# Group statistics by channel tiles on two engines, zeroing moved ahead, and a bias product moved behind the first products

## The chip, the cores and the metric

The kernel runs on one core of a Trainium2 chip. The time is the device time of one execution in microseconds. Engines are named as in the profile: PE (TensorE), DVE (VectorE), ACT (ScalarE), POOL (GpSimd) and SP, whose queue issues most of the DMAs.

## What is computed

Two layers on x of 384 channels by 192 by 192 pixels, in float32. Only the first half of the first layer bears on this change:

```python
def _gn(v, G=32, eps=1e-5):
    g = v.reshape(B_, G, C_ // G, H_, W_)
    m = jnp.mean(g, axis=(2, 3, 4), keepdims=True)
    s = jnp.var(g, axis=(2, 3, 4), keepdims=True)
    return ((g - m) / jnp.sqrt(s + eps)).reshape(v.shape)

x = x + L0(_gn(x))      # layer 0
x = x + L1(_gn(x))      # layer 1

# in L0, on h = _gn(x):
qkv = einsum('bchw,oc->bohw', h, w_qkv) + b_qkv      # 3*384 outputs
qkv = 2x2 max pool(qkv)                              # 96 x 96
qkv = depthwise 3x3 conv(qkv, w_dw) + b_dw
q, k, v = split(qkv)
attn = normalised q @ normalised k, over channels of a head
out = sum of four top-k softmaxes of attn @ v, gelu, repeat 2x2, projection
```

Layer 1 takes the sign of the normalised x, shifts channels by up to three columns and multiplies by the sign of a weight.

## The kernel before, in words

x is cut into 24 units of 8 image rows; a unit is 128 partitions by 3 channel tiles by 1536 pixels, 2304 KB. Units live in the pool "big" of eight slots (line 156), and `unit(u)` (lines 177 to 182) loads one by a DMA on SP's queue, or by three, one for each channel tile, with `parts=CT`.

Phase 1 (lines 219 to 294) streams all units, from 23 down to 0, and takes the statistics of the group norm. Every third unit goes to ACT whole: for each of its three channel tiles one pass that sums and one that sums the squares (line 239), into `acc`. The other units go to DVE whole: nine `bn_stats` of 512 pixels (line 248), and after every fourth such unit a `bn_aggr` for each tile (line 250). The last two units, 1 and 0, are both DVE's. Units 5 to 0 stay in their slots (`KEEP`). In between, nine matmuls of the group indicator with the weights (line 256) give `wg`, which ACT copies out (line 259). At the end DVE joins both kinds of partial sums (lines 263 to 269), PE adds them up by group (`group_sums`, line 198), a string of one-column steps makes mean and reciprocal deviation (lines 274 to 280), and `spread` (line 203) brings them back to channels. Then DVE scales the weights `wq` by the reciprocal deviation (line 287), nine matmuls of one column make the shift that the mean brings to the bias (line 293, "bqps"), and DVE adds it to `bq` (line 294). The normalised x is never written: the products take x itself, with the scaled weights.

Phase 2 (lines 353 to 436) makes q and k, unit by unit from 0 up. `qkv_unit` (lines 313 to 346) does one block of 128 output channels: three groups of three matmuls into a PSUM bank each (line 321, "qkv"; the pool has three banks), each group reduced by DVE's max pool (line 328) into a zero-bordered tile "pooled"; then ACT adds the bias `bq` (line 335) and begins the depthwise sum (line 342), and DVE adds eight more terms (line 344). DVE transposes the result in 32 by 32 blocks into "blocks" (line 383), DMAs on SP's queue move these into "room" (lines 396 and 401), a tile in one of the eight slots, and PE adds the products of q and k over pixels (line 412, "gram"), one unit behind. POOL zeroes "blocks" (line 361) and the borders of the six pooled tiles (lines 302 to 305) at the start of this phase.

Later phases make v, the softmaxes and the attention (lines 571 to 660), and the projection, layer 1 and the stores (from line 665); the change does not touch their code. One small step of theirs, a group sum of the projection's bias (lines 630 and 631, "bg"), depends on nothing but a constant.

The order within an engine's queue is set by a scheduler that works from the program's dependencies, outside the blocks marked `manual_schedule`; the engines then run their queues in order. Pools give out memory; a tile waits until what lay there before has been read.

Of the kernel before, what the change touches and what calls it, by code (L numbers as in the profile page):

```python
# [10 lines left out]
F32 = mybir.dt.float32  # L11
# [3 lines left out]
BF16 = mybir.dt.bfloat16  # L15
# [5 lines left out]
P = 128  # L21
# [126 lines left out]
def conv_preact_kernel(ctx: ExitStack, tc: tile.TileContext, a: dict, out: bass.AP):  # L148
# [58 lines left out]
    def right(name, bufs=1, stack=att):  # L207
        return stack.enter_context(tc.tile_pool(name=name, bufs=bufs, side="right"))
# [4 lines left out]
    gsb = ap.tile([P, CT, max(DN)], F32, name="gsb")  # L213
    osum = ap.tile([P, CT, NAB], F32, name="osum")
    aT = right("aT").tile([P, CT, C], F32, name="aT")
    wq = right("wq").tile([P, CT, 3 * C], F32, name="wq")


    kept = {}
    with tc.tile_pool(name="p1", bufs=1, side="right") as p1, tc.tile_pool(name="p1ps", bufs=2, space=PSUM) as psp:  # L220
        stats = [p1.tile([P, CT, BATCH * (UPX // 512) * 6], F32, name=f"stats{i}") for i in range(NB)]
        mv = p1.tile([P, CT, NB, 2], F32, name="mv")
        acc = p1.tile([P, CT, 2, NU // SHARE], F32, name="acc")
        wg = p1.tile([NG, 3 * C], F32, name="wg")
        seen = 0
        for i in range(NU):
            u = NU - 1 - i
            xt = unit(u, parts=CT if u in (0, NU - 1) else 1)
            if u < KEEP:
                kept[u] = xt  # L230
            if i == 0:
                nc.scalar.dma_start(small, a["small"])
                nc.scalar.dma_start(indT, a["indT"])
                nc.scalar.dma_start(wq, a["w_qkvT"].rearrange("(t p) o -> p t o", p=P))
            if i % SHARE == 0:
                for t in range(CT):
                    for k, f in enumerate((AF.Identity, AF.Square)):
                        junk = p1.tile([P, UPX], BF16, name="junk")
                        nc.scalar.activation(  # L239
                            junk, xt[:, t], f, accum_out=acc[:, t, k, i // SHARE : i // SHARE + 1]  # L240
                        )
            else:
                b, k = divmod(seen, BATCH)
                seen += 1
                for t in range(CT):
                    for j in range(UPX // 512):
                        at = (k * (UPX // 512) + j) * 6
                        nc.vector.bn_stats(stats[b][:, t, at : at + 6], xt[:, t, j * 512 : (j + 1) * 512])  # L248
                    if k == BATCH - 1:
                        nc.vector.bn_aggr(mv[:, t, b, :], stats[b][:, t, :])  # L250
            if u == NU // 2:

                for m in range(3):
                    ps = psp.tile([NG, C], F32, name="wgps")
                    for t in range(CT):
                        nc.tensor.matmul(
                            ps, ind[:, t, :], wq[:, t, m * C : (m + 1) * C], start=(t == 0), stop=(t == CT - 1)
                        )
                    nc.scalar.copy(wg[:, m * C : (m + 1) * C], ps)

        sums = p1.tile([P, CT, 2], F32, name="sums")
        more = p1.tile([P, CT, 2], F32, name="more")
        nc.vector.tensor_reduce(more, acc, AX.X, ALU.add)
        sq = p1.tile([P, CT, NB], F32, name="sq0")
        nc.vector.tensor_mul(sq, mv[:, :, :, 0], mv[:, :, :, 0])
        nc.vector.tensor_add(sq, sq, mv[:, :, :, 1])
        nc.vector.tensor_reduce(sums[:, :, 0], mv[:, :, :, 0], AX.X, ALU.add)
        nc.vector.tensor_reduce(sums[:, :, 1], sq, AX.X, ALU.add)
        nc.vector.scalar_tensor_tensor(sums, more, 1.0 / (BATCH * UPX), sums, ALU.mult, ALU.add)  # L269
        ps = psp.tile([NG, 2], F32, name="gsps")  # L270
        group_sums(ps, sums)

        gs = p1.tile([NG, 2], F32, name="gs")
        nc.vector.tensor_scalar_mul(gs, ps, BATCH / (NU * GRP))
        gv = p1.tile([NG, 2], F32, name="gv")
        nc.vector.tensor_scalar_mul(gv[:, 0:1], gs[:, 0:1], -1.0)
        var = p1.tile([NG, 1], F32, name="var")
        nc.vector.scalar_tensor_tensor(var, gs[:, 0:1], gv[:, 0:1], gs[:, 1:2], ALU.mult, ALU.add)
        nc.vector.tensor_scalar_add(var, var, 1e-5)
        inv_sqrt(p1, gv[:, 1:2], var, 1, "s0", NG)  # L280
        ps = psp.tile([P, CT, 2], F32, name="spread")
        spread(ps, gv)
        nc.vector.tensor_copy(rstd0, ps[:, :, 1])

        for c0, c1 in ((0, P), (P, 2 * C), (2 * C, 3 * C)):
            for t in range(CT):
                nc.vector.tensor_scalar_mul(wq[:, t, c0:c1], wq[:, t, c0:c1], rstd0[:, t : t + 1])
        nc.vector.tensor_copy(nmean0, ps[:, :, 0])
        shift = p1.tile([NG, 1], F32, name="shift")
        nc.vector.tensor_mul(shift, gv[:, 0:1], gv[:, 1:2])  # L290
        ps = psp.tile([P, NM], F32, name="bqps")
        for m in range(NM):
            nc.tensor.matmul(ps[:, m : m + 1], wg[:, m * P : (m + 1) * P], shift, start=True, stop=True)
        nc.vector.tensor_add(bq, bq, ps)  # L294

    def padded(pool, n):

# [8 lines left out]
            ts.append(t)  # L306
        return ts

    def rows(u):

        return (1 if u else 2), (PR if u < NU - 1 else PR + 1)

    def qkv_unit(pqkv, xt, u, m, pl, parts):


        x4 = xt.rearrange("p t (r w) -> p t r w", w=W)
        lo, hi = rows(u)
        for r0, nr, c0, ncol in BLOCKS:
            ps = pqkv.tile([P, 512], F32, name="qkv")
            for t in range(CT):  # L320
                nc.tensor.matmul(  # L321
                    ps,
                    wq[:, t, m * P : (m + 1) * P],
                    x4[:, t, r0 : r0 + nr, c0 : c0 + ncol],
                    start=(t == 0),
                    stop=(t == CT - 1),
                )
            nc.vector.tensor_reduce(  # L328
                pl[:, 2 + r0 // 2 : 2 + (r0 + nr) // 2, 1 + c0 // 2 : 1 + (c0 + ncol) // 2],
                ps.rearrange("p (i a j b) -> p i j a b", a=2, b=2, j=ncol // 2),  # L330
                AX.XY,
                ALU.max,
            )
        new = pl[:, 2 : 2 + PR, 1 : 1 + WP]
        nc.scalar.activation(new, new, AF.Identity, bias=bq[:, m : m + 1])  # L335
        for acc, r0, n in parts:
            acc2 = acc.rearrange("p (r w) -> p r w", w=WP)
            for k in range(9):
                r = lo - 1 + r0 + k // 3
                src = pl[:, r : r + n, k % 3 : k % 3 + WP]  # L340
                if k == 0:
                    nc.scalar.activation(acc2, src, AF.Identity, bias=bdw[:, m : m + 1], scale=wdw[:, m, 0:1])  # L342
                else:
                    nc.vector.scalar_tensor_tensor(acc2, src, wdw[:, m, k : k + 1], acc2, ALU.mult, ALU.add)  # L344
        if u < NU - 1:
            nc.scalar.copy(pl[:, 0:2, :], pl[:, PR : PR + 2, :])  # L346
# [3 lines left out]
    pqkv = products_of_x.enter_context(tc.tile_pool(name="qkv", bufs=3, space=PSUM))  # L350
    last_products = products_of_x.enter_context(ExitStack())
    pg = last_products.enter_context(tc.tile_pool(name="p2g", bufs=1, space=PSUM))
    with tc.tile_pool(name="p2w", bufs=1, side="right") as wp, tc.tile_pool(
        name="p2t", bufs=2, side="right"
    ) as tp:
        gram = [pg.tile([P, 512], F32, name=f"gram{t}") for t in range(CT)]


        size = -(-(PR + 1) * WP // P) * C
        blocks = wp.tile([P, 2, size], F32, name="blocks")  # L360
        nc.gpsimd.memset(blocks, 0.0)
        pool = padded(wp, 2 * CT)
        room = big.tile([P, CT, UPX], F32, name="room", tag="big").rearrange("p t n -> p (t n)")
        qkT = room[:, : 2 * size].rearrange("p (s n) -> p s n", s=2)

        def of_unit(u):
# [53 lines left out]
        for u in range(NU):  # L420
# [6 lines left out]
            n = hi - lo + 1  # L427
            for m in range(2 * CT):
                acc = tp.tile([P, (PR + 1) * WP], F32, name="dw")[:, : n * WP]
                qkv_unit(pqkv, xt, u, m, pool[m], [(acc, 0, n)])  # L430
                transposed(u, *divmod(m, CT), acc)
                sq = tp.tile([P, (PR + 1) * WP], BF16, name="sq", bufs=1)
                nc.scalar.activation(sq[:, : n * WP], acc, AF.Square, accum_out=ssq[:, m, u : u + 1])  # L433
                if u and m == CT - 1:
                    products(u - 1)
                if m % CT == CT - 1:
                    moved(u, m // CT)
# [420 lines left out]
```

## Time and profile before

| | |
|---|---|
| median of 4 runs | 2287.62 us (2287.54 to 2289.3) |
| the profiled execution | 2287.57 us, span 2285.8 us |
| mean granted clock of PE | 0.965 |
| x loads of the first stage | 25 units' worth, 58.98 MB, on SP's queue until 165 us; the DMA engines move 410 to 425 GB/s without a gap until 150 us |
| first product (L321) | 160.86 us |
| bn_stats (L248) | 144, 676 ns each by their records |
| ACT's passes (L239) | 48, 1482 ns each, and a read of the sum after each |
| bqps (L293) | 18 records, from 156.63 on, 3.97 us |
| POOL's zeroing of "blocks" (L361) | 2.66 us, from 160.72 on |

A float32 matmul stands in the trace as two records, so nine matmuls are 18. In the profile "L321 qkv<-xt,wq" means: line 321 writes qkv from xt and wq. In the slices each digit is a fortieth of the span (57 us), in tenths busy; PEclk is the clock that was granted to PE, in tenths of full speed. In the timeline the bracket behind a row gives how long the engine had been idle before it and what ended that. In the windows the columns after the length are the busy times of PE, PE's weight loads, DVE, ACT and POOL with their counts, then the granted clock, the DMA share and GB/s.

### The profile page before, as it was taken

The page shows a single profiled execution, that of the slowest core. Times are in us where ns is not written, and L with a number is a line of the kernel's source. Part 1 is how long each engine was busy: PE and PEld are TensorE (multiplying, and loading weights), DVE is VectorE, ACT ScalarE, POOL GpSimd, SP SyncE. Part 2 cuts the span into 40 slices and gives each one's busy share as a digit, 9 for nine tenths or more (in the row PEclk, how much of TensorE's full clock was granted, in tenths as well). Part 3 has the DMA queues.
Part 4 walks back from the last instruction along what each step waited for, and adds up shares of the span by engine and source line. Part 5 has one row for each costly group of instructions (what it writes and reads, how often), then busy time and mean ns, then how long its engine had stood idle before and what let it go on. Part 6 is the DMA issues. An engine that isn't in the chain of part 4 may idle for free.

```text
span 2285.8 us, 19474 instructions
## 1 busy us (share of the span) xinstructions
PE 2101.0 (92%) x6135; PEld 993.5 (43%) x6135; DVE 1903.1 (83%) x3269; ACT 819.4 (36%) x1418; POOL 211.9 (9%) x338
## 2 busy tenths in 40 slices
PE   1029999999999999999999979999999999989998
PEld 0014444444444444444444434444444444445554
DVE  4667888888888888888888878986787887889998
ACT  5532222222222222222222212225323233487775
POOL 0000000000000000000000000000000000276674
PEclk7559999999999999999999989999999999999999
DMA  9962222232222232222232222104222212289996
GB/s 398 418 261 61 65 64 70 69 98 70 66 64 71 69 98 70 65 64 70 70 96 71 65 48 84 41 24 183 83 83 73 93 42 83 83 334 404 421 413 249
DMA packets 208727, 300.30 MB, mean 131 GB/s; under 512 B 162000, under 2 KB 164848, under 8 KB 208624
## 3 DMA queue, kind: packets, MB, share of 16 engines
q1 hardware_dynamic: 197936, 243.46, 30.7%
q10 hardware_dynamic: 10688, 55.61, 6.0%
q8 instruction: 48, 0.79, 0.1%
q14 instruction: 55, 0.45, 0.1%
HBM read 213.68 MB, written 56.62 MB: 118 GB/s over the span
## 4 chain that ended last, share of the span: by engine, by line
PE 75%; DVE 12%; DMA 8%; ACT 2%; issue 1%; SPq 1%; ACTq 0%; POOLq 0%; POOL 0%; DVEq 0%
PE qkv L321 63%; DMA xt<-in_x_dram 7%; DVE chunk L344 5%; PE l1ps L743 4%; PE yps L559 3%; PE gram L412 3%; DVE pooled L328 2%; PE ops L594 2%; DVE xt L568 2%; DVE dw L344 1%; ACT signs L723 1%; DVE stats L248 1%; DMA out_dram<-xt 1%; ACT chunk L342 0%; ACT pooled L335 0%
## 5 line engine op out<-in xcount | busy, mean ns | idle before, releaser
L321 PE MATMUL qkv<-xt,wq 128*128 128x512 f32 x3888 | 1682.5, 594 | 0.3 <-DVE small L294 0.3
L321 PEld LDWEIGHTS qkv<-xt,wq 128*128 128x128 f32 x3888 | 736.7, 190 | 920.5 <-issue 824.6
L344 DVE SCALAR_TENSOR_TENSOR dw<-pooled,small,dw 128x384 f32<-128x384 f32 (+2 forms) x1152 | 708.9, 615 | 118.8 <-ACT dw L342 93.7
L328 DVE TENSOR_REDUCE pooled<-qkv 128x128 f32<-128x512 f32 x648 | 442.5, 684 | 72.3 <-PE qkv L321 71.8
L344 DVE SCALAR_TENSOR_TENSOR chunk<-pooled,small,chunk 128x384 f32<-128x384 f32 (+3 forms) x696 | 370.1, 545 | 74.7 <-ACT chunk L342 57.3
L346 ACT COPY pooled<-pooled 128x196 f32<-128x196 f32 x207 | 73.7, 356 | 764.4 <-DVE dw L344 543.0
L335 ACT ACTIVATE pooled<-pooled,small 128x384 f32<-128x384 f32 x216 | 133.0, 616 | 408.1 <-DVE pooled L328 400.6
L723 ACT ACTIVATE signs<-xt,nmean 64x1536 fp8e4<-64x1536 f32 x144 | 226.5, 1573 | 62.0 <-PE yps L559 50.7
L743 PE MATMUL l1ps<-signs,wb 128*128 128x384 fp8e4 x864 | 150.6, 329 | 5.7 <-POOL signs L715 4.5
L568 DVE SCALAR_TENSOR_TENSOR xt<-yps,small,xt 128x768 f32<-128x768 f32 x132 | 127.8, 1012 | 24.3 <-PE yps L559 19.7
L559 PE MATMUL yps<-chunk,wpr 128*128 128x384 f32 x396 | 136.5, 490 | 6.6 <-DVE xt L568 6.6
L751 DVE SCALAR_TENSOR_TENSOR xt<-l1ps,small,xt 128x768 f32<-128x768 f32 x144 | 135.6, 1008 | 6.3 <-ACT signs L723 4.0
L248 DVE BATCH_NORM_STATS2 stats<-xt 128x6 f32<-128x512 f32 x144 | 87.2, 676 | 60.4 <-DMA xt<-in_x_dram 60.4
L198 PE MATMUL gsps<-sums,small 128*32 128x2 f32 x6 | 0.5, 196 | 127.9 <-DVE sums L269 127.9
L433 ACT ACTIVATE sq<-dw 128x384 bf16<-128x384 f32 (+2 forms) x144 | 75.3, 523 | 117.0 <-DVE dw L344 117.0
L743 PEld LDWEIGHTS <-wb 128*128 128x128 fp8e4 x864 | 84.1, 97 | 73.4 <-issue 15.5
L302 POOL MEMSET pooled<- 128x196 f32 x9 | 2.4, 269 | 1172.2 <-DVE dw L344 1154.8
L342 ACT ACTIVATE dw<-pooled,small 128x384 f32<-128x384 f32 (+2 forms) x144 | 100.5, 698 | 2.3
L559 PEld LDWEIGHTS yps<-chunk,wpr 128*128 128x128 f32 x396 | 72.7, 190 | 62.0 <-PE yps L559 15.6
L239 ACT ACTIVATE junk<-xt 128x1536 bf16<-128x1536 f32 x48 | 71.1, 1482 | 51.4 <-DMA xt<-in_x_dram 50.3
L383 DVE STREAM_TRANSPOSE blocks<-dw 128x384 f32<-128x384 f32 (+1 forms) x144 | 82.0, 569 | 3.4
L412 PE MATMUL gram<-room 128*128 128x160 f32 (+3 forms) x438 | 68.1, 309 | 15.3 <-DMA room<-blocks 15.3
(117 smaller groups left out, 641.3 us busy)
## 6 DMA issues: line engine op xcount, KB each, us to landing
xt<-in_x_dram SPq DMA_DIRECT2D x83, 2304.0 KB, 12.6
out_dram<-xt ACTq DMA_DIRECT2D x19, 2304.0 KB, 14.5
room<-blocks SPq DMA_DIRECT2D x736, 36.0 KB, 2.0
xt<-in_x_dram SPq DMA_DIRECT2D x18, 768.0 KB, 8.6
out_dram<-xt ACTq DMA_DIRECT2D x9, 768.0 KB, 8.3
out_dram<-xt SPq DMA_DIRECT2D x6, 768.0 KB, 6.6
wq<-in_w_qkvT_dram ACTq DMA_DIRECT2D x1, 1728.0 KB, 14.9
room<-blocks SPq DMA_DIRECT2D x32, 48.0 KB, 2.1
```

The lines of the kernel that those rows point to most:

```text
L248: nc.vector.bn_stats(stats[b][:, t, at : at + 6], xt[:, t, j * 512 : (j + 1) * 512])
L321: nc.tensor.matmul(ps, wq[:, t, m * P : (m + 1) * P], x4[:, t, r0 : r0 + nr, c0 : c0 + ncol], start=(t == 0), stop=(t == CT - 1),)
L328: nc.vector.tensor_reduce(pl[:, 2 + r0 // 2 : 2 + (r0 + nr) // 2, 1 + c0 // 2 : 1 + (c0 + ncol) // 2], ps.rearrange("p (i a j b) -> p i j ...
L335: nc.scalar.activation(new, new, AF.Identity, bias=bq[:, m : m + 1])
L342: nc.scalar.activation(acc2, src, AF.Identity, bias=bdw[:, m : m + 1], scale=wdw[:, m, 0:1])
L344: nc.vector.scalar_tensor_tensor(acc2, src, wdw[:, m, k : k + 1], acc2, ALU.mult, ALU.add)
L412: nc.tensor.matmul(gram[t][:, : BN[t] * B], q[:L, t, i], k[:L, B0[t] : B0[t] + BN[t], i], start=u == 0 and i == 0, stop=u == NU - 1 and i ...
L559: nc.tensor.matmul(ps, wpr[:, t, m * P : (m + 1) * P], o[:, t, :], start=(t == 0), stop=(t == CT - 1),)
L568: nc.vector.scalar_tensor_tensor(x5[:, m, r], yb, bpr[:, m : m + 1], x5[:, m, r], ALU.add, ALU.add)
L723: nc.scalar.activation(rows_of(sg, p, SAT[t] - HSHIFT[t][h]), xt[p, t, :].rearrange("p (r w) -> p r w", w=W), AF.Sign, bias=nmean1[p, t : ...
L743: nc.tensor.matmul(ps[:, j, : 2 * W], wb[:, t, m * P : (m + 1) * P], rows_of(sg, slice(0, P), SAT[t])[:, r0 + 2 * j : r0 + 2 * j + 2], sta ...
L751: nc.vector.scalar_tensor_tensor(blk, ps[:, :, : 2 * W], bl1[:, m : m + 1], blk, ALU.add, ALU.add)
```

## The change

- Statistics: of every unit one channel tile (number u modulo 3) goes to ACT and two go to DVE; both write into one tile `part`, ACT with its scale folded in, and one column of `part` carries the epsilon. The joining becomes a square, an add and one reduction; one scaling reads the sums from PSUM directly, and the step that added epsilon is gone. Unit 1 is loaded in three DMAs as well.
- Memory: the partial statistics and ACT's throwaway output lie in "room", which is now taken from the eight slots ahead of the stream; `wg` lies in `aT`, a tile of a later phase, and `shift` in a pool of its own.
- Zeroing: "blocks" and the six pooled tiles are allocated and zeroed ahead of the statistics.
- Bias: the nine matmuls and the add are a function that `qkv_unit` calls once, for unit 0 and block 0, behind the nine products and their three reductions, into a fourth tile of the product pool.
- The scheduler also moves "bg": its three matmuls and its DVE step now stand at the front of their queues. Otherwise the queues keep their order from the first products on.

```diff
+    wg = aT.rearrange("p t c -> p (t c)")[:NG]
+    shift = ap.tile([NG, 1], F32, name="shift")
...
-        stats = [p1.tile([P, CT, BATCH * (UPX // 512) * 6], F32, name=f"stats{i}") for i in range(NB)]
-        mv = p1.tile([P, CT, NB, 2], F32, name="mv")
-        acc = p1.tile([P, CT, 2, NU // SHARE], F32, name="acc")
-        wg = p1.tile([NG, 3 * C], F32, name="wg")
...
+    blocks = wp.tile([P, 2, size], F32, name="blocks")
+    nc.gpsimd.memset(blocks, 0.0)
+    padded_qk = padded(wp, 2 * CT)
+    room = big.tile([P, CT, UPX], F32, name="room", tag="big").rearrange("p t n -> p (t n)")
...
+        stats = [room[:, i * size1 : (i + 1) * size1].rearrange("p (t n) -> p t n", t=CT) for i in range(NB)]
+        junk = room[:, NB * size1 : NB * size1 + UPX // 2].bitcast(BF16)
+
+        part = p1.tile([P, CT, 2, NB + NU // SHARE + 1], F32, name="part")
+        measure = 1.0 / (BATCH * UPX)
+        nc.vector.memset(part[:, :, 0, NB + NU // SHARE :], 0.0)
+        nc.vector.memset(part[:, :, 1, NB + NU // SHARE :], 1e-5 * NU / BATCH)
...
-            xt = unit(u, parts=CT if u in (0, NU - 1) else 1)
+            xt = unit(u, parts=CT if u in (0, 1, NU - 1) else 1)
...
-            if i % SHARE == 0:
-                for t in range(CT):
-                    for k, f in enumerate((AF.Identity, AF.Square)):
-                        junk = p1.tile([P, UPX], BF16, name="junk")
-                        nc.scalar.activation(
-                            junk, xt[:, t], f, accum_out=acc[:, t, k, i // SHARE : i // SHARE + 1]
-                        )
-            else:
...
+            for t in range(CT):
+                if t == u % SHARE:
+                    at = NB + i // SHARE
+                    for k, f, scale in ((0, AF.Identity, measure), (1, AF.Square, measure**0.5)):
+                        nc.scalar.activation(junk, xt[:, t], f, scale=scale, accum_out=part[:, t, k, at : at + 1])
+                    continue
+                b, k = divmod(seen[t], BATCH)
+                seen[t] += 1
+                for j in range(UPX // 512):
+                    at = (k * (UPX // 512) + j) * 6
+                    nc.vector.bn_stats(stats[b][:, t, at : at + 6], xt[:, t, j * 512 : (j + 1) * 512])
+                if k == BATCH - 1:
+                    nc.vector.bn_aggr(part[:, t, :, b], stats[b][:, t, :])
...
-        nc.vector.tensor_reduce(more, acc, AX.X, ALU.add)
...
-        nc.vector.tensor_reduce(sums[:, :, 0], mv[:, :, :, 0], AX.X, ALU.add)
-        nc.vector.tensor_reduce(sums[:, :, 1], sq, AX.X, ALU.add)
-        nc.vector.scalar_tensor_tensor(sums, more, 1.0 / (BATCH * UPX), sums, ALU.mult, ALU.add)
...
+        nc.vector.tensor_mul(sq, part[:, :, 0, :NB], part[:, :, 0, :NB])
+        nc.vector.tensor_add(part[:, :, 1, :NB], part[:, :, 1, :NB], sq)
+        nc.vector.tensor_reduce(sums, part, AX.X, ALU.add)
...
-        nc.vector.tensor_scalar_mul(gv[:, 0:1], gs[:, 0:1], -1.0)
+        nc.vector.tensor_scalar_mul(gv[:, 0:1], ps[:, 0:1], -BATCH / (NU * GRP))
...
-        nc.vector.tensor_scalar_add(var, var, 1e-5)
...
-        ps = psp.tile([P, NM], F32, name="bqps")
-        for m in range(NM):
-            nc.tensor.matmul(ps[:, m : m + 1], wg[:, m * P : (m + 1) * P], shift, start=True, stop=True)
-        nc.vector.tensor_add(bq, bq, ps)
...
+    def bias(ps):
+
+        for m in range(NM):
+            nc.tensor.matmul(ps[:, m : m + 1], wg[:, m * P : (m + 1) * P], shift, start=True, stop=True)
+        nc.vector.tensor_add(bq, bq, ps)
...
+        if before:
+            before(pqkv.tile([P, 512], F32, name="qkv")[:, :NM])
         new = pl[:, 2 : 2 + PR, 1 : 1 + WP]
         nc.scalar.activation(new, new, AF.Identity, bias=bq[:, m : m + 1])
...
-                qkv_unit(pqkv, xt, u, m, pool[m], [(acc, 0, n)])
+                qkv_unit(pqkv, xt, u, m, padded_qk[m], [(acc, 0, n)], None if u or m else bias)
```

## The prediction, as put on record

> **What bounds it now.** I read the page first (busy shares, slices, chain of work), then the chain of waits in order of time for the first 260 us, then the timeline of that stretch engine by engine, then busy time by windows. On the page TensorE decides: 75% of the chain. The slices show the one stretch where it does not, the first two, in which the DMA row is full and PE all but empty.
>
> ```profile
> PE 2101.0 (92%) x6135; PEld 993.5 (43%) x6135; DVE 1903.1 (83%) x3269; ACT 819.4 (36%) x1418; POOL 211.9 (9%) x338
> ...
> PE   1029999999999999999999979999999999989998
> ...
> PEclk7559999999999999999999989999999999999999
> DMA  9962222232222232222232222104222212289996
> ```
>
> In order of time the chain of this stretch reads (start, length, what): x is streamed in, the statistics lag behind it, a string of tiny steps follows, then two groups of small matmuls, then the products.
>
> ```profile
> 109.44 30.59 DMA xt<-in_x_dram
> 140.03 0.02 issue
> 140.06 7.81 DVE stats L248 x13
> ...
> 155.33 1.44 PE spread L203 x6
> 156.76 3.85 PE bqps L293 x18
> ...
> 160.86 72.60 PE qkv L321 x164
> ```
>
> From 160.86 on PE has no gap: between 300 and 1300 it is busy 1000 us of 1000 while DVE has 128 us to spare. So what starts the products earlier moves everything behind them by the same amount, and PE work added among them is paid in full.
>
> ```profile
> 300.00:1300.00 1000.00, 1000.00 (x2570) 471.68 (x2570) 871.69 (x1472) 265.19 (x614) 0.00 (x0) 1.00 0.26 74
> ```
>
> VectorE's timeline at the end of the stream (start, length, what, idle before):
>
> ```profile
> 128.77 5.44 DVE L248 BATCH_NORM_STATS2 stats<-xt 128x6 f32<-128x512 f32 x9 [0.21 <-DMA xt<-in_x_dram]
> 140.06 7.81 DVE L248 BATCH_NORM_STATS2 stats<-xt 128x6 f32<-128x512 f32 x13 [5.85 <-DMA xt<-in_x_dram]
> ...
> 151.53 0.48 DVE L250 BATCH_NORM_AGGREGATE mv<-stats 128x2 f32<-128x72 f32 x1
> 152.05 0.17 DVE L265 TENSOR_TENSOR sq<-mv 128x12 f32<-128x12 f32 x1
> ...
> 157.00 3.05 DVE L287 TENSOR_SCALAR wq<-wq,rstd 128x128 f32<-128x128 f32 x9
> ```
>
> DVE idles 5.85 us while ScalarE has unit 2, then gets units 1 and 0 whole, and works through their 18 statistics without a pause until 152: units come every 5.64 us ((140.03-128.77)/2, unit 2 between), so unit 0 lands near 140.03+5.64 = 145.7, long before DVE is done with it.
>
> **Part 1, statistics by channel tile.** Each unit now gives ScalarE one tile (two passes at 1.61 us from start to start, 3.2 us) and DVE two (6 bn_stats at 5.44/9 = 0.604, 3.6 us). Both are under 5.64, so both keep up and the last pieces to land decide. Units 1 and 0 come in thirds, 5.64/3 = 1.88 apart: unit 0's tiles 0, 1, 2 at about 141.9, 143.8, 145.7. DVE: tile 1 from 143.8, three bn_stats 1.81 and an aggregate (0.38 to the next start) until 146.0; tile 2 then 1.74, its aggregate at 147.7, and 0.52 later (151.53 to 152.05 above) the squares at 148.3. Gain 152.05-148.3 = **3.8**. ScalarE has tile 0 and is done at 141.9+3.2 = 145.1; its table load (1.28 in the trace) ends at 146.4, three microseconds before the square root needs it: nothing.
>
> **Part 2, the tiny steps.** Squares to group sums took 0.83 (152.05 to 152.88); now squares, add, one reduce at 0.20+0.21+0.25 = 0.66. From the evicted sums (153.39) to the root (154.16) 0.77; now the second scaling follows the first without waiting (0.08, as the copy at 156.88 does behind that at 156.80), then 0.18, then 0.24: 0.50. Gain **0.4**.
>
> **Part 3, bias behind the first products.** After the spread PE need only wait for the first scaled block of wq: scaling starts at 157.00, its first 128 columns take some 0.2 (an estimate: 3.05 us for nine of 3456 columns in all), so products could start at 157.25 and not at 160.86. Gain **3.6**. The nine bias matmuls (18 records) come back after the ninth product of unit 0, PE being the bound there. Their price before is 3.97/18 = 0.22 each at a granted clock of 0.50; the same shape at full clock stands near the end:
>
> ```profile
> 1984.44 0.82 PE L203 MATMUL p3ps<-gm,indT 32*128 32x1 f32 x6
> 1985.20 2.20 PE L559 MATMUL yps<-chunk,wpr 128*128 128x384 f32 x6
> ```
>
> Six in 0.76 is 0.127 each, so 18 x 0.127 = **2.3 lost**. They can't run cold: the first nine products lasted until 170.8, ten microseconds, and the clock was full four after their start. [...] The trace has 0.22 and 0.127 by clock; I take the row. [...] at most it is the cold 4.0.
>
> Who waits for it: in VectorE's queue the bias add stands between the third reduction and the depthwise steps of the first tile, and ScalarE's bias activation waits for the add. Against the first product, the depthwise steps began at 172.99-160.86 = 12.1; now 10.0 (nine products) + 2.3 + add 0.2 + the two activations 1.4 = 13.9. They slip 1.8 while PE slips 2.3, so PE still finds its bank free: the bias borrows one of three banks, whose reduction ended about 5.5 after the start.
>
> **Part 4, moves at no cost.** GpSimd's zeroing (160.72 to 165.7) goes to the front, where that queue is idle; DVE's first reduction waited for PE then, not for it. One DVE and three PE instructions for bg move from 1344 to the front; DVE's sits in a chain there that ends in the wait for the transposes: gain **0.1** (1344.58 to 1344.70). At the front DVE's bg waits for the small load (landed 5.68) with the bn_stats behind it; ScalarE's three copies of the weight sums wait for PE (to 25.1 before) with the statistics of units 22 on behind them, a backlog of two tiles, 6.5 us, which a surplus of 2.4 per unit clears in three units. SP issues two more transfers (unit 1 in thirds); the DMA engines, not the issue, are full. "room" holds one of eight slots from the start, so seven carry the stream: rival D.
>
> **Clock.** Before, the clock rose 3.96 us after the first product:
>
> ```profile
> 163.00:164.00 1.00, 1.00 (x2) 0.40 (x2) 0.00 (x0) 0.00 (x0) 1.00 (x9) 0.50 0.00 0
> 164.00:165.00 1.00, 1.00 (x2) 0.34 (x1) 0.00 (x0) 0.00 (x0) 1.00 (x12) 0.59 0.00 0
> 165.00:166.00 1.00, 1.00 (x4) 0.46 (x3) 0.31 (x1) 0.00 (x0) 0.70 (x8) 1.00 0.00 0
> ```
>
> The bias matmuls ahead of it did not warm it (0.50 throughout), so by the row their removal costs nothing and the cold stretch stays 3.96. [...] I take the row, 0[...].
>
> **Sum.** 3.8+0.4+3.6-2.3+0.1 = 5.6 to 5.7. The profiled execution took 2287.57 (span 2285.8), the median is 2287.62, so no correction: 2287.6-5.7 = **2281.9**. What is late next: the last third of unit 0, i.e. the stream itself.
>
> **Rivals.** A measurement here tells about 0.2% from no change, 4.6 us.
> A, as worked: 2281.9, give or take 1.2. Chance 0.66.
> B, the bias loads hide under products (cost 0.5) : 2280.1. For: a 128-column load mostly hides under its neighbour in the product rows. Against: the row of six at 0.127 is at full clock and does not hide. 0.12.
> C, the stream gives part back: transfers of unit 0 and of the reload of unit 6 behind it overlap (DMA ran on to 150.2), and if the last third lands one third later, 1.9 is lost: 2283.8[...]. Against: unit landings 5.6 to 5.7 apart all along. 0.18; within 0.2%.
> D, slower: with seven slots the stream starves while ScalarE is held by the copies. For: a slot is now freed only by two engines, and unit 15 needs that of unit 22. Against: ScalarE is free at about 25.5 and done with unit 22's tile at 28.8, when units 19 to 16 and the rest of 20, over 22 us of transfer, are still queued. It decides only if ScalarE is held until about 50, and must cost 10.3 to end above 2292: 2293. 0.04.
> That the move does not happen is excluded by the built order: nine products, nine bias matmuls, then 73 products.
>
> Faster by over 0.2% (below 2283.0): 0.95 of A, and B, 0.75; within: the rest of A, and C, 0.21; slower: D, 0.04. The range 2280.0 to 2284.4 covers A, most of B and of C.
>
> **What would show it.** Unit 0's last bn_stats after a DMA wait, squares near 148.3; first product near 153.0; bias group 2.3 long some 10 after it, no PE wait for a bank behind it; idle before 1359 unchanged; all later stages shifted by one constant. Wrong if the first product moves and the end does not, if DMA share dips before 145, or if DVE waits for ScalarE at the sums.

## The result and the profile after

| | before | after |
|---|---|---|
| median | 2287.85 us (2285.42 to 2291.18, 55 runs) | 2283.52 us (2281.57 to 2286.72, 35 runs) |
| profiled execution, span, clock | 2287.57, 2285.8, 0.965 | 2282.50, 2280.7, 0.966 |

The ratio is 0.9982, 95% interval 0.9977 to 0.9987: 4.1 us less (3.0 to 5.3). The medians differ by 4.3. The range held the result, and the predicted 2281.9 lies 1.6 below the median. The 0.2% that the prediction set between "faster" and "within" lies inside the interval; by the median, 2283.52 for its limit of 2283.0, it came out "within", to which the prediction had given 0.21. One thing was in none of the cases: the 35 times of after stand in two groups, 23 from 2281.57 to 2283.90 (median 2283.1) and 12 from 2284.93 to 2286.72 (median 2285.8). The times of before form one group. Single executions that took far longer (two of again, one each of dist, reused2 and before) are left out of every median and spread below.

Page of after, the slices of PE and of its clock: the third slice is a tenth fuller in both rows and one slice near the end of PE's is too, the rest is as before, so the page alone does not tell the story.

```profile
PE   1039999999999999999999979999999999999998
...
PEclk7569999999999999999999989999999999999999
```

Chain of waits of after, in order of time (start, length, what):

```profile
121.98 21.71 DMA xt<-in_x_dram
143.72 1.89 DVE room L276 x3
...
148.40 0.18 DVE sq L290
...
151.34 1.45 PE spread L203 x6
153.04 0.46 DVE wq L309 x2
153.55 9.82 PE qkv L331 x18
163.37 2.09 PE qkv L316 x18
165.47 62.85 PE qkv L331 x146
```

From the last wait for the stream to the squares it is now 4.7 us, before 12 (140.03 to 152.05). The squares start at 148.40 (foreseen 148.3). The product starts at 153.55, not 153.0: the spread before it starts 0.2 later than foreseen, and two scalings (0.46) stand ahead of the product. The bias group is where it was meant to be, 2.09 long.

VectorE's timeline of after shows that the pieces of unit 0 are waited for, and that the nine scalings still take 3.05 in all, though PE no longer waits for the last of them. GpSimd's timeline has the zeroing at the front of the kernel.

```profile
143.72 1.88 DVE L276 BATCH_NORM_STATS2 room<-xt 128x6 f32<-128x512 f32 x3 [1.73 <-DMA xt<-in_x_dram]
...
153.01 3.05 DVE L309 TENSOR_SCALAR wq<-wq,rstd 128x128 f32<-128x128 f32 x9
```

```profile
0.87 2.66 POOL L241 MEMSET blocks<- 128x3072 f32 x1
```

Windows of after (busy PE, PE's loads, DVE, ACT, POOL, then the clock): a mean of 0.85 is half clock for 0.30 of this microsecond, so full clock came at 157.30, after a cold stretch of 3.75.

```profile
157.00:158.00 1.00, 1.00 (x3) 0.48 (x2) 0.00 (x0) 0.00 (x0) 0.00 (x0) 0.85 0.00 0
```

Then the shift against before, read at the same instruction of both profiles: spread 3.99 earlier, first product 7.31, first gram 5.13, second cold start 5.37, a row of the attention near 1927 4.77, the spread of the last stage 4.77, last matmul group 4.92. It is not one constant, as the prediction had it. The step from 5.37 to 4.77 is the second cold stretch, behind an idle time that did not change (15.32, in before 15.27): from the restart of PE to full clock it took 5.11, in before 3.84. The two restarts in PE's timelines, after and then before, and the windows in which the clock rose (at 1358.79 and 1362.90):

```profile
1353.68 0.87 PE L415 MATMUL gram<-room 128*128 128x160 f32 x2 [15.32 <-DMA room<-blocks]
```

```profile
1358.00:1359.00 1.00, 1.00 (x2) 0.38 (x2) 0.18 (x1) 0.35 (x1) 0.00 (x0) 0.60 0.14 22
```

```profile
1359.05 0.87 PE L412 MATMUL gram<-room 128*128 128x160 f32 x2 [15.27 <-DMA room<-blocks]
```

```profile
1362.00:1363.00 1.00, 1.00 (x2) 0.34 (x1) 1.00 (x2) 0.00 (x0) 0.00 (x0) 0.55 0.00 0
```

And PE's timeline of the last stage has a wait that before does not have; in before, "yps" follows the three spread matmuls without a gap.

```profile
1979.67 0.82 PE L203 MATMUL p3ps<-gm,indT 32*128 32x1 f32 x6
1981.87 4.11 PE L562 MATMUL yps<-chunk,wpr 128*128 128x384 f32 x12 [1.37 <-DVE nmean L663]
```

In this execution the wait cost nothing: from that spread to the last matmul group it took 287.48, in before 287.63.

### The profile page after: what moved, and what is told of

Its sections match the earlier page's. It is cut to its first block, busy times and chain, and to the rows that moved or that the text cites. A ratio compares the mean times of both kernels' runs of the same rounds, so it can differ in the third digit from the quotient of the medians.

```text
span 2280.7 us, 19487 instructions
## 1 busy us (share of the span) xinstructions
PE 2099.8 (92%) x6135; PEld 992.0 (43%) x6135; DVE 1904.3 (83%) x3267; ACT 819.8 (36%) x1418; POOL 211.9 (9%) x338
## 4 chain that ended last, share of the span: by engine, by line
PE 75%; DVE 12%; DMA 8%; ACT 2%; issue 1%; SPq 0%; ACTq 0%; POOLq 0%; POOL 0%; DVEq 0%
PE qkv L331 63%; DMA xt<-in_x_dram 7%; DVE chunk L356 5%; PE l1ps L746 4%; PE yps L562 3%; PE gram L415 3%; DVE pooled L338 2%; PE ops L597 2%; DVE xt L571 2%; DVE dw L356 1%; DMA out_dram<-xt 1%; ACT signs L726 1%; ACT chunk L354 0%; ACT pooled L347 0%; SPq L404 0%
## 5 line engine op out<-in xcount | busy, mean ns | idle before, releaser
L276 DVE BATCH_NORM_STATS2 room<-xt 128x6 f32<-128x512 f32 x144 | 88.1, 677 | 49.1 <-DMA xt<-in_x_dram 49.1
L270 ACT ACTIVATE room<-xt 128x1536 bf16<-128x1536 f32 x48 | 71.2, 1483 | 55.3 <-DMA xt<-in_x_dram 54.5
```

## The experiments

Two questions: where the foreseen 5.7 shrank, and what makes the second group. Times of all kernels (ratios are against before, measured beside each):

| kernel | median, us | spread, runs | ratio |
|---|---|---|---|
| again | 2285.22 | 2282.53 to 2286.6, 18 | 0.9985 (0.9978 to 0.9992) |
| dist | 2285.71 | 2284.68 to 2286.65, 20 | 0.9988 (0.9981 to 0.9995) |
| twice | 2289.21 | 2286.74 to 2291.62, 13 | 1.0002 (0.9994 to 1.001) |
| ahead | 2284.44 | 2283.03 to 2285.71, 17 | 0.9984 (0.9976 to 0.9991) |
| halves | 2283.81 | 2282.43 to 2285.11, 13 | 0.9981 (0.9973 to 0.9989) |
| biasonly | 2291.39 | 2289.18 to 2293.37, 19 | 1.0013 (1.0006 to 1.002) |
| reused | 2283.56 | 2281.22 to 2286.22, 18 | 0.9978 (0.9971 to 0.9985) |
| reused2 | 2283.93 | 2282.34 to 2286.08, 20 | 0.9982 (0.9976 to 0.9989) |
| turned | 2287.89 | 2284.62 to 2289.42, 13 | 0.9997 (0.9989 to 1.0005) |
| latezero | 2286.38 | 2285.15 to 2288.66, 13 | 0.9992 (0.9984 to 1.0) |

**First theory: the clock falls behind the bias group.** It rested on the bias matmuls of before, which did not warm the clock (0.50 in all of their 3.97 us): behind the products they might let it fall. How often, for how long and at what cost was the author's estimate.

again, the changed kernel without an edit.

> The changed kernel unchanged. Its 35 executions fall into two groups: 24 from 2281.6 to 2283.9 and 11 from 2284.9 to 2286.7. Theory 1 (the clock falls back): [...] It expects two groups again, near 2282.9 and 2285.8, about a third in the upper one, and in a profile of the upper group a granted clock of 0.5 somewhere between 165 and 180 us. Theory 2 (cold starts only): the upper group is made of executions whose two cold starts (first products, 1354 us) are both long; it expects full clock from 161 us to 1340 us in every profile.

Nine of 18 lie from 2285.75 up, so the group is real (in the 35 times above it is 23 and 12, not 24 and 11). The profile of again, of an execution of 2605.61 us, says nothing about it; two more profiles of after follow as again2 and again3.

dist, the nine columns spread over six blocks, one or two each:

```diff
-        for m in range(NM):
+        for m in ms:
...
-        nc.vector.tensor_add(bq, bq, ps)
+            nc.vector.tensor_add(bq[:, m : m + 1], bq[:, m : m + 1], ps[:, m : m + 1])
...
-                qkv_unit(pqkv, xt, u, m, padded_qk[m], [(acc, 0, n)], None if u or m else bias)
+                qkv_unit(pqkv, xt, u, m, padded_qk[m], [(acc, 0, n)], None if u else lambda ps: bias(ps, (m, 6 + m) if m < 3 else (m,)))
```

> The nine bias matmuls are no longer one group: one or two columns stand among the products of each of the six blocks of unit 0, 0.12 to 0.25 us at a time. PE's work is the same. Theory 1 expects the upper group to go, and a median near that of the lower group, 2282.9 plus or minus 0.5. Theory 2 expects the same two groups and a median of 2283.5.

PE's timeline of dist:

```profile
164.00 0.38 PE L316 MATMUL qkv<-shift,aT 32*128 32x1 f32 x2
164.31 1.98 PE L331 MATMUL qkv<-xt,wq 128*128 128x512 f32 x4
166.22 0.38 PE L316 MATMUL qkv<-shift,aT 32*128 32x1 f32 x2
```

One group, as the theory wanted, but 2.8 above its figure. A lone column takes 0.31 from start to start (164.00 to 164.31), and the four product records behind it take 1.91 (to 166.22) where 62.85/146 = 0.43 each, as in after's chain, makes 1.72: another 0.19. So 0.5 for a lone column, 0.23 for one in a group: each interruption of the products costs about 0.27 of its own. All nine columns stand alone in PE's timeline, so they make 4.5 for the 2.4 of one interrupted group, which is 2.1 of the 2.8.

twice, each column made twice, 36 records:

```diff
-        for m in range(NM):
+        for m in (*range(NM), *range(NM)):
```

> The bias group is computed twice in a row behind the first products (36 records in place of 18), into the same columns. Both theories expect the second nine to cost 18 x 0.116 = 2.1 us. Theory 1 expects [...] median 2287.3 (2286.5 to 2288.5), and a granted clock of 0.5 behind the group in the profile. Theory 2 expects 2285.6 and full clock there.

Windows of twice, right behind a group of 4.17 us:

```profile
167.00:168.00 1.00, 1.00 (x7) 0.92 (x7) 0.16 (x1) 0.18 (x1) 0.00 (x0) 0.81 0.00 0
168.00:169.00 1.00, 1.00 (x2) 0.34 (x1) 0.00 (x0) 0.92 (x2) 0.00 (x0) 0.50 0.03 8
```

Here the clock does fall behind the group, at 167.6, and stays at 0.5 until 171, though PE counts as fully busy. The median, 2289.21, is above what either theory gave, and the same profile has a second fall, 1986.9 to 1990.3, in the last stage, together with the wait of 1.37. That is the place that decides, as the next runs show.

ahead, the changed kernel with the bias group ahead of the first products as in before:

```diff
+        ps = psp.tile([P, NM], F32, name="bqps")
+        for m in range(NM):
+            nc.tensor.matmul(ps[:, m : m + 1], wg[:, m * P : (m + 1) * P], shift, start=True, stop=True)
+        nc.vector.tensor_add(bq, bq, ps)
...
-                qkv_unit(pqkv, xt, u, m, padded_qk[m], [(acc, 0, n)], None if u or m else bias)
+                qkv_unit(pqkv, xt, u, m, padded_qk[m], [(acc, 0, n)])
```

> The changed kernel with only the bias group and its add put back ahead of the first products; statistics, small steps and zeroing stay as changed. Products should start some 3.3 us later than in the changed kernel (at 156.8) and not be interrupted for 2.1. Theory 1 expects one group without a fall of the clock behind the start, near 2282.9 + 3.3 - 2.1 + 0.1 = 2284.2, so that the move of the bias is worth about 1.2 us where the clock holds and costs 1.5 where it falls, 0.4 on the mean. Theory 2 expects a median 1.2 us above the changed kernel's, 2284.7, with the same two groups.

One group, no wait, and no fall of the clock behind the spread of the last stage; its spread of the statistics starts at 151.45 for 155.33. All of the change but the bias's move brings 4.0 (2288.40, before beside it, to 2284.44). The lower group of after is 4.75 below its own before (2287.85 to 2283.1), so there the bias's move adds some 0.8. In the medians it is not shown to pay: the ratio is 0.9984 here, 0.9982 for after and 0.9985 for again, which ran beside it.

**Two more profiles of after**, unchanged.

> The changed kernel once more, for the profile of one execution. Theory 1 (the clock falls back behind the bias group) expects, if the time is above 2284.9, a granted clock of 0.5 for 3.4 us between 165 and 172 us; if it is below 2284, full clock there. Theory 2 (cold starts only) expects full clock there in both cases, and the difference in the length of the cold stretches at the first product and at 1354 us.

> As the run before: a second execution of the changed kernel, with the same expectations by its time.

2286.78 and 2286.82, both of the upper group. The clock is full right behind the bias group (1.00 from 158 on): the first theory is wrong about the place. Everything up to the last stage's spread stands within 0.35 us of the first profile of after, and that spread within 0.25. PE's timeline of again2, then its windows:

```profile
1982.12 7.74 PE L562 MATMUL yps<-chunk,wpr 128*128 128x384 f32 x18 [1.37 <-DVE nmean L663]
```

```profile
1983.00:1984.00 1.00, 1.00 (x4) 0.55 (x3) 0.00 (x0) 0.97 (x2) 0.16 (x1) 0.74 0.00 0
1984.00:1985.00 1.00, 1.00 (x3) 0.58 (x2) 0.00 (x0) 1.00 (x1) 0.84 (x2) 0.50 0.03 8
```

18 records at after's 0.34 each (4.11/12) make 6.2; they took 7.74. The clock is at one half for 3.41 us (0.74, 0.50, 0.50, 0.55 over four slices), 1.6 us of products are lost, and the stage ends 4.0 later: 291.51 from spread to last group for 287.48. PE itself makes the 1.6 good: its first products behind the wait for GpSimd start 23.50 after the spread in both profiles. What stays late, counted from the spread, is the way through memory: the first store is issued 1.7 later (2000.39 for 1998.44) and so is the first reload into the freed slots (2003.83 for 2001.89), the piece that VectorE needs comes 3.0 later, and PE waits for VectorE. PE's timelines of again2 and of after:

```profile
2024.19 4.88 PE L746 MATMUL l1ps<-signs,wb 128*128 128x384 fp8e4 x18 [5.85 <-DVE xt L754]
```

```profile
2020.92 3.11 PE L746 MATMUL l1ps<-signs,wb 128*128 128x384 fp8e4 x18 [1.16 <-DVE xt L754]
```

Around that wait the clock of again2 is at one half once more, from 2021.0 to 2027.9 (these 18 records take 4.88 for 3.11), where after has one such stretch, from 2003.9 to 2007.3. Why a reload that is issued 1.7 later lands 3.0 later is not taken apart.

**Second theory: the banks.** Why the wait of 1.37? The bias takes one tile more from the pool of three banks, and the pool goes round. The last stage's "yps" tiles lie where that pool lay, and by the theory one extra turn puts the first of them into the bank whose last reader (DVE, line 571) is still at work until 1981.72. VectorE's timeline of after:

```profile
1979.78 1.94 DVE L571 SCALAR_TENSOR_TENSOR xt<-qkv,small,xt 128x768 f32<-128x768 f32 x2 [0.61 <-PE qkv L562]
1981.64 0.15 DVE L663 TENSOR_TENSOR nmean<-nmean,p3ps 128x3 f32<-128x3 f32 x1
```

PE's row names the step that ended last, "nmean"; but the product starts 0.15 after the end of line 571, as it does behind the two later waits for that line. Kernels with 0, 2 or 6 extra tiles (before, ahead, halves, dist) should be free of the wait; of the profiles already there, dist has six, ahead none, twice one: they agree.

halves, five columns behind block 0 and four behind block 1, two extra tiles:

```diff
-                qkv_unit(pqkv, xt, u, m, padded_qk[m], [(acc, 0, n)], None if u or m else bias)
+                qkv_unit(pqkv, xt, u, m, padded_qk[m], [(acc, 0, n)], None if u or m > 1 else lambda ps: bias(ps, (0, 5)[m], (5, NM)[m]))
```

> The bias matmuls stand in two groups, five columns behind the nine products of block 0 (1.2 us) and four behind those of block 1 (0.9 us). An interruption of the products costs about 0.27 beside its own matmuls (0.5 for one column in the run with the columns spread singly, 0.116 a record within a group), so the sum of PE's work is 0.3 more than in the changed kernel. Theory 1 expects [...] no upper group: one group from 2282 to 2284.5, median 2283.2, against 2283.5 to 2285.7 for the changed kernel. Theory 2 expects the changed kernel's two groups, 0.3 later.

One group, no wait, no fall behind the spread; the two groups of columns are 1.27 and 1.05 long.

biasonly, the kernel of before with only the bias moved (`wg`, `shift`, `bias` and the hook in `qkv_unit` as in the change; statistics and zeroing as before).

> The kernel before with only the bias group moved behind the first nine products (and wg and shift laid elsewhere for that); statistics by whole units and the small steps stay as before. By the sum: products 3.3 earlier, 2.1 + 0.3 lost, so 0.9 to 1.0 below the kernel before where the clock holds, and 0.8 or more above it where it falls. Theory 1 expects two groups, near 2287.3 and 2290, and a median not clear of the kernel before (ratio 0.9995 to 1.0005). Theory 2 expects 0.9 below: ratio 0.9996, one group as wide as the kernel before. Both: with the run in which the bias stands ahead (4.0 below the kernel before), the parts add up to the changed kernel.

It is slower than before, by 3.0 us (2288.35 beside it), outside what was expected: an effect that neither theory had. Timelines of VectorE, GpSimd and PE in biasonly, and GpSimd's in before:

```profile
156.94 5.50 DVE L288 TENSOR_SCALAR wq<-wq,rstd 128x128 f32<-128x128 f32 x9
```

```profile
156.83 2.66 POOL L365 MEMSET blocks<- 128x3072 f32 x1 [155.52 <-PE spread L203]
```

```profile
159.82 9.40 PE L323 MATMUL qkv<-xt,wq 128*128 128x512 f32 x18 [3.11 <-DVE wq L288]
```

```profile
160.72 2.66 POOL L361 MEMSET blocks<- 128x3072 f32 x1 [159.41 <-PE bqps L293]
```

The nine scalings by line (shortest, median, longest in ns), in biasonly and in after:

```profile
L288 DVE TENSOR_SCALAR wq<-wq,rstd x9: 357/540/2621, 156.9 to 162.0; 128x128 f32<-128x128 f32 x3, 128x640 f32<-128x640 f32 x3, 128x384 f32<-128x384 f32 x3
```

```profile
L309 DVE TENSOR_SCALAR wq<-wq,rstd x9: 278/410/544, 153.0 to 155.6; 128x128 f32<-128x128 f32 x3, 128x640 f32<-128x640 f32 x3, 128x384 f32<-128x384 f32 x3
```

The zeroing waits for the memory of the first phase. In before that memory was held by the bias group until 160.72; with the group gone it comes free at the spread, and the zeroing falls on the scaling. One scaling took 2621 ns, about the length of the zeroing, and the first products wait for it: 3.11, where they wait 0.78 in after. The zeroing began first (156.83, then 156.94), and nearly all of the loss is one stall about as long as the zeroing (2.66); by what the one holds up the other is not shown. The nine scalings lose 2.45, more than the 0.9 to 1.0 that the bias's move was expected to win. The difference, 1.5, is what the seven lowest executions (2289.18 to 2290.28) stand above before; the others are later still. This kernel has one extra tile, and its profile has the wait of 1.37 and a fall of the clock from 1988.9 to 1992.3 as well.

latezero asks the same of the changed kernel: the zeroing back behind the statistics.

```diff
-    pairs = ctx.enter_context(ExitStack())
-    wp = right("p2w", stack=pairs)
-    size = -(-(PR + 1) * WP // P) * C
-    blocks = wp.tile([P, 2, size], F32, name="blocks")
-    nc.gpsimd.memset(blocks, 0.0)
-    padded_qk = padded(wp, 2 * CT)
...
+    pairs = ctx.enter_context(ExitStack())
+    wp = right("p2w", stack=pairs)
+    size = -(-(PR + 1) * WP // P) * C
+    blocks = wp.tile([P, 2, size], F32, name="blocks")
+    nc.gpsimd.memset(blocks, 0.0)
+    padded_qk = padded(wp, 2 * CT)
     def bias(ps):
```

> The changed kernel with the zeroing of the blocks and of the pooled tiles put back behind the statistics, so that GpSimd does it while VectorE scales the weights. Theory (the scaling of the first products' weights is stretched by the zeroing, as in the kernel in which only the bias was moved): the nine scalings take 5 to 5.5 us in place of 3.05, the first products stretch by about 2.5 us, and the time is 2 to 3 us above the changed kernel: ratio to before 0.9992 to 0.9998, near 2286 for the lower group of executions. Rival (the prediction's: the zeroing has room wherever it stands and moving it is worth nothing): 2282.5 to 2283.5 and ratio 0.9978 to 0.9982, as the changed kernel.

Timelines of GpSimd, VectorE and PE in latezero:

```profile
153.21 2.66 POOL L311 MEMSET blocks<- 128x3072 f32 x1 [151.91 <-PE spread L203]
```

```profile
153.33 5.81 DVE L303 TENSOR_SCALAR wq<-wq,rstd 128x128 f32<-128x128 f32 x9
```

```profile
156.40 10.40 PE L332 MATMUL qkv<-xt,wq 128*128 128x512 f32 x18 [3.31 <-DVE wq L303]
```

The nine scalings take 5.81, one of them 2818 ns, and the first products start at 156.40 for 153.55. The lower of two groups stands at 2286.0, 2.4 above reused (below), which ran beside it. So the zeroing's place is worth 2.4 to 2.85, more than the bias's move brings: without it that move would cost time.

turned, "ahead" with one lone extra column in a tile of its own, so that the banks are turned though the bias is not moved:

```diff
+        nc.tensor.matmul(ps[:, 0:1], wg[:, 0:P], shift, start=True, stop=True)
+        nc.vector.tensor_copy(spare, ps[:, 0:1])
```

> The kernel with the bias group ahead of the first products (one group of executions, 2284.44), plus one lone extra bias column behind the first block in a tile of its own, whose result goes to a spare tile and is not used. It turns the pool's banks by one without moving the bias group. Theory (bank rotation): the last stage's product shows the wait of about 1.37 us again; the lone column itself costs about 0.5, so the lower group lies near 2284.9, and some executions, up to half, lie 3 to 4 us above, 2288 to 2289; median 2285 to 2288. Rival (the bias group's place makes the second group): one group at 2284.9 and no fall of the clock in the last stage.

PE's timeline of turned:

```profile
1982.44 0.82 PE L203 MATMUL p3ps<-gm,indT 32*128 32x1 f32 x6
1984.63 7.74 PE L567 MATMUL yps<-chunk,wpr 128*128 128x384 f32 x18 [1.37 <-DVE nmean L668]
```

The wait is back with one column, and the clock falls (0.50 from 1985.9 to 1989.3). The median is 3.4 above ahead, of which the column itself explains 0.5. The theory expected up to half of the executions above; it was most of them, without a clear gap.

reused, the other half of the pair: the bias group stays behind the first products, but is written into the second product's tile, already reduced, so that no extra tile is taken.

```diff
+        used = []
...
+            used.append(ps)
...
-            before(pqkv.tile([P, 512], F32, name="qkv")[:, :NM])
+            before(used[1][:, :NM])
```

> The changed kernel with one difference: the nine bias columns are written behind the first block's third product as before, but into the second product's tile of the same block, which VectorE has already reduced, so that no extra tile is taken from the three-bank pool. Theory (the odd extra tile turns the pool's banks, so that the last stage's first product finds its bank taken, and on some executions the clock is halved for one 3.4-us window there): the 1.37-us wait of the last stage's fourth product and the fall of the clock near 1984 are gone; the executions form one group near the lower group of the changed kernel, 2282.5 (2281.5 to 2283.9), ratio to before 0.9975 to 0.9979. Rival (the second group comes from the bias group's place behind the first products[...]): two groups remain, the upper 3 to 4 us above the lower, and a fall near 1984 stays possible.

PE's timeline of reused:

```profile
1981.05 0.82 PE L203 MATMUL p3ps<-gm,indT 32*128 32x1 f32 x6
1981.81 4.14 PE L564 MATMUL yps<-chunk,wpr 128*128 128x384 f32 x12
```

No wait, and no fall behind the spread; 17 of 18 executions lie from 2281.22 to 2284.69. The ratio, 0.9978, was as expected; to size the one at 2286.22 the kernel was run again.

> The bias in the second product's tile once more, unchanged, to size the rarer group. Theory (the turned banks were the cause): again one group near 2283.5 and at most one execution in ten above 2285; ratio to before 0.9976 to 0.9981, so that with the first call it lies below the changed kernel's 0.9982. Rival (the single group of the first call was luck, and this kernel has the second group too): a third or more of the executions lie 3 us or more above the lower ones, and the ratio is 0.9982 to 0.9986. A fall of the clock in the last stage in its profile would speak for the rival.

A miss for the theory's figure: 5 of 20 are above 2285, with no gap between them and the rest, at 0.9982. The profile again has neither the wait nor the fall behind it. So the banks explain the separate upper group, but not all of the scatter. What the profiles of reused and reused2 show is the cold stretch of the first products: 4.85 and 5.96 long for 3.75 in after's, and the second one, from 1355, 5.4 and 5.9 for 5.1. The granted clock is 0.50 in it, so half of such a stretch is lost, which makes 0.7 and 1.5 of the 1.3 and 2.3 us by which these executions are longer; a start 0.36 and 0.23 later is part of the rest, and 0.3 and 0.5 stay open. Taken together 6 of 38 executions of reused lie above 2285 and 20 of 53 of the changed kernel. By the ratios (0.9978 and 0.9982 against 0.9982 and 0.9985, intervals of 0.0005 and more on either side) it is not shown to be the faster kernel.

What stands: of the seven profiles of kernels with one extra tile (after, again2, again3, twice, biasonly, turned, latezero) all have the wait, and five have the fall behind it; the two without, after and latezero, are executions of their lower group. Of the six without that turn (before, dist, ahead, halves, reused, reused2) none has either. All eight profiles without this fall have one of 3.41 us later, some 24 us behind the spread, at the wait for GpSimd; before has it too.

**Which executions fall.** The traces' clock records answer this for the profiles at hand. In all thirteen, every change of the clock lies a whole number of 3.413 us from the one before it (in after 347 of them from the rise at 157.30 to the fall at 1341.72, in again2 one from the fall at 1983.48 to the rise at 1986.90), so the changes lie on a grid, and the grid lies differently against the kernel in each profile. The first grid point behind the wait of the last stage came so long after the wait's end:

| | fell | did not fall |
|---|---|---|
| us from the wait's end to the next grid point | 1.15 (biasonly), 1.26 (turned), 1.33 (again3), 1.36 (again2), 1.36 (twice) | 1.56 (after), 1.66 (latezero) |

In the 3.41 us before that point PE counts as busy for 2.04 in all seven; but for 0.1 at most, what is not products behind the wait is the one-column matmuls of the spread. So what sorts the seven is how much of wide products stood in that stretch. ahead is the control: it has no wait, its grid point lies 3.48 us behind the start of the spread, among the 3.35 to 3.56 of the five that fell, and its clock holds:

```profile
1981.59 0.82 PE L203 MATMUL p3ps<-gm,indT 32*128 32x1 f32 x6
1982.35 4.14 PE L566 MATMUL yps<-chunk,wpr 128*128 128x384 f32 x12
```

The same holds for every stretch from one grid point to the next, 8589 of them from 20 us on in the thirteen profiles, if only matmuls of 128 columns and more are counted: at full clock it fell behind 1.36 us of them or less and held behind 1.56 or more; at half clock it rose behind 2.91 or more and stayed behind 2.80 or less. With the matmuls of one and two columns counted in, no such limit exists: it fell behind 3.41 (twice) and held behind 2.04 (after). Behind the bias group the nearest to a fall was reused2, with 1.56.

That this also sorts the executions without a profile is inferred.

## Why the prediction was right, and where it was not

**Statistics and tiny steps: right.** Foreseen 3.8 + 0.4 by the start of the spread, measured 3.65 + 0.34 = 3.99 in the profiles, and 4.0 in ahead's median. The small steps ahead of the group sums took 0.78, not 0.66: three dependent steps start 0.20, 0.29 and 0.29 apart.

**First product: 0.3 too early.** From spread to product the foreseen gain was 3.6, measured 3.32 (5.53 to 2.21). One scaling lasts 0.28, not 0.2, and the product's first start came after the second of them. The larger point is what this step rested on: part 4's zeroing "goes to the front" at no cost was argued from GpSimd's queue being idle there. It is right that it costs nothing there; that it would cost 2.4 to 2.85 where the bias's move leaves it was not seen. The step came out because the change has both parts, and in so far it was luck.

**Bias group: right in size, blind to the distance.** Foreseen 2.3, measured 2.09, plus the 0.27 that an interruption costs in dist: 2.36. No wait for a bank followed it, as argued; but the step that named the borrowed bank looked only at the blocks next to it, and the wait came 1820 us later. Rival B, loads that hide, whose cost of 0.5 no row had shown, is refuted by the same row.

**The clock: not the row's constant.** The row gave a constant 3.96. The first cold stretches are 3.75 (after), 3.64, 3.42 (again2, again3), 4.85, 5.96 (reused, reused2), 4.91 (latezero), 5.37 (ahead), 6.21 (turned) and 2.91 (biasonly), and the second one of dist is 3.05. Each ends on the grid, and a stretch of the grid was not always busy from end to end when the clock rose: 2.91 us of products sufficed (biasonly) and 2.80 did not (turned), as above. In the profiled after the first stretch gave 0.1 and the second, 5.11 for 3.84, took 0.6.

**Where the rest went.** In the profiles: 3.99 + 3.32 - 2.36 + 0.10 (half of 3.96 - 3.75) = 5.05, where the shift at the first gram is 5.13. By the second cold start it is 5.37 (0.1 was foreseen for "bg" on the way), the second cold stretch takes it to 4.77, and in the times of the two executions it is 5.07 (2287.57 to 2282.50). The failed step is "all later stages shifted by one constant". It left out two things, the second cold start, for which the prediction took 0, and the last stage, which meets its banks one turn later and loses 2.7 in 12 of 35 executions (2285.8 for 2283.1). Of the foreseen 5.7 the medians show 4.3. Of the missing 1.4, 0.6 is missing in the profiles already, nearly all of it the second cold stretch; 0.4 is the second group, which moves the median from 2283.1 to 2283.5; and 0.3 is where the two profiled executions lie, 0.6 below the median of after's lower group and 0.3 below that of before.

C and D did not happen: the last third had landed by 146.03, where its statistics start without a wait, and no part of the stream starves.

Open: why a reload of the last stage that is issued 1.7 us later lands 3.0 later, whether the grid also sorts the executions without a profile, and which other step scatters in reused2.

## What to carry to other kernels

A tile added to a rotating pool is a change at every later place that draws from it: compare the waits of far stages as well as those next to the edit, and reuse a tile that is already read where one will do. When a wait is taken away, ask what else was released by it: here the bias group had been keeping GpSimd's zeroing off VectorE's scaling (the nine take 3.05 us in before and 5.50 in biasonly). And look at the single times ahead of the median: two groups mean that one profile shows only one of two stories.

## What the runs showed of the hardware

- In all thirteen profiles the clock changed only on a grid of 3.413 us, and the grid lay differently against the kernel from profile to profile.
- Matmuls of one column didn't hold the clock up, though PE counts as busy: behind 36 records in 4.17 us, which filled the 3.41 us before the fall, it fell to 0.5 for 3.41 us (twice). Behind 18 in 2.1 us it did not, in any profile.
- What sorts the stretches of 3.413 us is how long matmuls of 128 columns and more ran in them. Full clock was kept behind 1.56 us and more and lost behind 1.36 and less, so a gap of 1.37 us with one-column matmuls beside it was enough (again2, again3, twice, biasonly, turned; held in after and latezero). Full clock came behind 2.91 us and more (biasonly) and not behind 2.80 and less (turned).
- Where a GpSimd zeroing of 2.66 us began just before VectorE's nine scalings, one of them took 2621 and 2818 ns, about the zeroing's length (biasonly, latezero); without it the longest took 544 (after).
- A column among products cost 0.5 us alone and 0.23 in a group of nine, so an interruption cost about 0.27 of its own (dist, after).
